# Loads, first sums, constants and the range flag: parts of a graph network kernel issued in another order

## The chip, the cores and the metric

The kernel runs on one core of one Trainium2 chip. A core has five engines, each with its own queue of instructions that it works through in order: TensorE (PE, matmul and transpose; its weight loads are listed as PEld), VectorE (DVE), ScalarE (ACT), GpSimd (POOL) and SyncE (SP, which only issues DMAs here). DMAs are issued from the queues of SP, ACT and POOL and moved by 16 DMA engines. A DMA's completion, and work on another engine, is waited for by a semaphore at the head of an instruction, and whatever stands behind that instruction on its engine waits too. The metric is the device time of one execution in microseconds (us), lower is better; of several executions the median is taken.

## What is computed

Sixteen graphs of 1024 nodes with 128 features, and a 0/1 adjacency `adj` of 1024 x 1024 each. Two layers, each with a residual and a normalization:

```python
# layer 0: a gated graph network of L = 4 steps
h = x
for i in range(L):
    hw = einsum('bnc,cd->bnd', h, weight[i])
    m  = einsum('bjn,bjd->bnd', adj, hw)
    h  = gru_cell(m, h, w_ih[i], w_hh[i], b_ih[i], b_hh[i])
x = layernorm(x + h * mask)

# layer 1: the adjacency is thinned row by row (each row's removals
# change later rows), then three SAGE layers and a linear head
adj_d = adj * dilate(adj > 0, mask)
def sage(x, Wr, Wx, b):
    agg = einsum('bij,bjd->bid', adj_d, x) / clip(sum(adj_d, -1), 1)
    out = agg @ Wr + x @ Wx + b
    return out / max(norm(out), 1e-12) * mask
h1 = bn(relu(sage(x,  Wr1, Wx1, b1)), g1, be1)     # bn: over all graphs and nodes
h2 = bn(relu(sage(h1, Wr2, Wx2, b2)), g2, be2)
h3 = bn(relu(sage(h2, Wr3, Wx3, b3)), g3, be3)
out = layernorm(x + (concat([h1, h2, h3]) * mask @ Wl + bl) * mask)
```

## The kernel before

P = C = 128, N = 1024, NB = 8 row tiles to a graph, HF = 512 columns (half a graph), B = 16 graphs, L0 = 4 GRU steps. A graph's adjacency is eight tiles of 128 x 1024 float32 (512 KB each). The order of the work on every engine is the order in which the program is written (a manual schedule for all five engines); the schedule adds the semaphore waits.

**The GRU pass** (`Gated`, to about 1329 us) works on two streams of graphs (even and odd), layer by layer in turn. A stream holds a graph's features as a high part and a low part (`hi`, `lo`: names h_hi, h_lo) so that sums over the adjacency are matmuls in a fast format; `layer` first makes the sums m = adj x (hi + lo) (line L1080, 32 matmuls of 128 x 512 into two banks, the first half of the columns, then the second), copies them (L1083), then makes the gates (L1092) with sigmoid, tanh and so on from ACT, DVE and POOL. `aside(n)` is called at fixed places in a layer and puts the other stream's work, and one step of the thinning, there. A stream's start for a graph is: load_x and load_adj (L1009, L1004, both from POOL's queue), `begin_rows` (hi by ACT L1044, lo by POOL L1045) and `begin(0)`, `begin(1)` (transposes of x, L1037).

**The thinning** (`FixPoint.steps`, a generator) is woven into it. A step loads four f_a tiles (L683, four graphs), takes their diagonal blocks (transposes L767 into f_pd), scans the rows on DVE (L735, prefix counts), derives parameters (L886 on ACT among them) and products (f_x, L893), and multiplies with f_tri on PE (L901). Further lines (L775, L863 and so on) repeat the removal for the block.

**The start** of the program: `make_consts` (identity, nodemask as nm_in, L613; mask, L618; first, L623), the first stream's x and eight h_a tiles on POOL's queue, all weights of the GRU on ACT's queue (`load_weights`, L953 to L961), four f_a tiles on SP's queue, `begin_rows`, then `prepare`: PE transposes every weight (L972, L975), multiplies (L979), and ACT and DVE copy the results. Weights of the four steps come in the tiles h_ms, h_r, h_z, h_zh. The second stream's x and h_a are then issued on POOL's queue, and `begin(0)` and the first nine steps of the thinning precede the first layer.

**The first Sage pass** (`Sage.first`, about 1329 to 1900) runs through slots (b, t), b = -1 to 15, t = 0 to 15. In a slot, unit (b + 1, t) of the next graph makes one of 16 blocks of the thinned adjacency (p_u, matmuls L1482, L1488, L1489 from p_nr and four p_a tiles; ACT makes p_at, L1490; POOL packs it, L1497), while for graph b PE aggregates (p_ag, L1561) and the layer follows. SP's queue carries the loads (p_nr L1466, p_a L1458, p_s L1472) and stores. `load_given` (20 loads of the Sage weights and vectors and three of the mask) is issued behind graph 0's loads. In slot (-1, 9) `constants` makes small tables on DVE and POOL: among them a copy of the identity (`drop`), and a row of ones that three DMAs store to rho (L1290). In slot (0, 1) `first_weights` multiplies the first Wr with drop (L1297), transposes the vectors (L1300) and copies the mask (mask48). A check on DVE (L1506) looks at each p_a tile for values that the fast way can't take, and writes to `bad`.

**The second and third passes** are the two further SAGE layers; in the third (about 2165 to 2286), iteration i takes up one unit (b, f), with transposes (L1411) of the unit three before. **The last part** (to 2365) makes the head and the normalization, graph by graph: eight blocks of 128 x 128 of a graph (k = 0 to 7; 0 to 3 from y in SBUF, 4 to 7 from one bank of PSUM) are scaled by POOL (k = 0), ACT (L1925) and, in the last graph, also DVE (L1923), and stored by SP (L1926).

**The flag.** `flagged` reduces `bad` on DVE (l_max), sums over partitions on PE (l_sum, L1964), makes 0 or 1 (l_flag, L1966), and every engine loads it to a register (L1967). If it is not 0, a general version would run; it is 0 here.

Of the kernel before, what the change touches and what calls it, by code (L numbers as in the profile page):

```python
# [8 lines left out]
F32 = mybir.dt.float32  # L9
# [12 lines left out]
P = 128  # L22
# [604 lines left out]
class FixPoint:  # L627
# [110 lines left out]
    def steps(self):  # L738

        nc, G = self.nc, self.G  # L740
        for c in range(G):
            self.load(c)
        old = None
# [173 lines left out]
class Gated:  # L917
# [27 lines left out]
    def load_weights(self):  # L945

        nc, wk = self.nc, self.wk
        weight, w_ih, w_hh, b_ih, b_hh = self.given
        self.w = wk.tile([P, 4, P], F32, name="h_w")
        self.w_in = {}  # L950
        names = iter(n for n in "h_ms h_r h_z h_zh".split() for _ in range(2))
        for l in range(L0):
            nc.scalar.dma_start(self.w[:, l, :], weight[l])  # L953
            for n, src in enumerate((w_ih, w_hh)):
                t = wk.tile([C, HF], F32, name=next(names))
                t = self.w_in[l, n] = t[:, :3 * C].rearrange("p (g c) -> p g c", g=3)
                nc.scalar.dma_start(t, src[l].rearrange("(g p) c -> p g c", p=C))
        t = wk.tile([P, NB, C], F32, name="h_x", bufs=3)
        self.b_in = [t[:L0 * 3, i, :] for i in range(2)]
        for t, src in zip(self.b_in, (b_ih, b_hh)):  # L960
            nc.scalar.dma_start(t, src.rearrange("l (g c) -> (l g) c", c=C))  # L961

# [28 lines left out]
    class Stream:  # L991
# [48 lines left out]
        def begin_rows(self, b):  # L1040
            x = self.x[b]
            for f in range(2):
                rows = slice(4 * f, 4 * f + 4)
                self.nc.scalar.copy(self.hi[:, rows, :], x[:, rows, :])  # L1044
                self.nc.gpsimd.tensor_tensor(self.lo[:, rows, :], x[:, rows, :],  # L1045
                                             self.hi[:, rows, :].bitcast(F32), ALU.subtract)

# [13 lines left out]

    def layer(self, st, l, aside):

# [5 lines left out]
        pm = [bank() for f in range(2)]  # L1069
        ms = []  # L1070
        for f in range(2):
            for n, part in enumerate((st.hi, st.lo)):
                if (f, n) != (0, 1):
                    aside(2 * f + n)
# [49 lines left out]
    def run(self, steps):  # L1124

        streams = [self.stream(s) for s in range(2)]
        first, second = streams
        first.load_x(first.b)
        for j in range(NB):
            first.load_adj(first.b, j)  # L1130
        self.load_weights()
        next(steps)
        first.begin_rows(first.b)
        self.prepare()
        second.load_x(second.b)
        for j in range(NB):
            second.load_adj(second.b, j)

        first.begin(0)
        for n in range(9):  # L1140
            next(steps)
        for b0 in range(0, B, 2):
            for l in range(L0):
                for s in range(2):
                    st, ot = streams[s], streams[1 - s]
                    self.layer(st, l, self.beside(st, ot, l, s, b0, steps))
        last = streams[1]
        for f in range(2):
            last.finish(f)
        for _ in steps:  # L1150
            pass
# [45 lines left out]
class Sage:  # L1197
# [61 lines left out]
    def constants(self):  # L1259
# [16 lines left out]
        nc.vector.memset(self.r6[:, C:], 0.0)  # L1276
        work = self.wk.tile([P, NB, C], F32, name="p_rl", bufs=1)

        mask, junk = self.cst["mask"], work[:, 0, :].rearrange("p (a b) -> p a b", a=NB)
        nc.vector.scalar_tensor_tensor(junk, mask, 0.0, mask, op0=ALU.is_gt, op1=ALU.not_equal,  # L1280
                                       accum_out=self.bad[:, BAD - 1:BAD])

        drop = work[:, 1, :]
        nc.vector.tensor_copy(drop, ident)
        nc.vector.memset(drop[:1, :], -1.0)
        nc.vector.memset(drop[:1, :1], 0.0)
        o = work[:B, 4:, :].bitcast(BF).rearrange("p a b -> p (a b)")
        nc.vector.memset(o, 1.0)
        for i in range(3):
            nc.sync.dma_start(self.rho[:, 3 + i, :], o)  # L1290
        self.drop = drop

    def first_weights(self):
        nc, ident = self.nc, self.cst["ident"]
        bank = lambda: self.ps1.tile([P, 4, P], F32, name="s_tr")[:, 0, :]
        w = bank()
        nc.tensor.matmul(w, self.drop, self.wr[:, 0, :], start=True, stop=True)  # L1297
        nc.vector.tensor_copy(self.wr[:, 0, :], w)
# [116 lines left out]
    def first(self):  # L1415

        nc, tc, cst = self.nc, self.tc, self.cst
        with ExitStack() as c:
# [22 lines left out]
            for k in range(4, NB):  # L1441
                self.load_a(0, k)
            self.load_given()
            self.eps = self.const([P, 1], 1e-5, "s_eps")
# [4 lines left out]
            for t, v in ((self.xh, 1.0), (self.xl, 0.0)):  # L1449
                nc.vector.memset(t[:, :, :1].bitcast(F32), v)  # L1450
            for b in range(-1, B):
                for t in range(16):
                    self.slot(b, t)
# [146 lines left out]
    def slot(self, b, t):  # L1600
# [82 lines left out]
        if nxt:  # L1683
            if t == 10:
                nc.sync.dma_start(self.at8[n, 0], self.g[n]["b", 0])
            if t == 13:
                nc.sync.dma_start(self.x1[n], self.g[n]["s"])
        if (b, t) == (-1, 9):
            self.constants()
        if (b, t) == (0, 1):  # L1690
            self.first_weights()
# [138 lines left out]
    def third(self):  # L1830

        nc, tc = self.nc, self.tc
        with ExitStack() as c:
# [9 lines left out]
            units = [(b, f) for b in range(B) for f in range(2)]  # L1843
            for i in range(len(units) + 3):

                if i >= 3:
# [20 lines left out]
    def last(self, r48):  # L1867
        nc, tc, cst = self.nc, self.tc, self.cst
        with ExitStack() as c:
# [42 lines left out]
            def norm(b):  # L1912
# [4 lines left out]
                for k in range(NB):  # L1917
                    src = pp[:, k - 4, :] if k > 3 else y[:, k, :]
                    scale, shift = rs[:, 0, k:k + 1], rs[:, 1, k:k + 1]
                    if k == 0:  # L1920
                        nc.gpsimd.tensor_scalar(y[:, k, :], src, scale, shift, op0=ALU.mult, op1=ALU.add)
                    elif b == B - 1 and k % 2 == 0:
                        nc.vector.tensor_scalar(y[:, k, :], src, scale, shift, op0=ALU.mult, op1=ALU.add)  # L1923
                    else:
                        nc.scalar.activation(y[:, k, :], src, AF.Identity, bias=shift, scale=scale)  # L1925
                nc.sync.dma_start(rows_of(self.out[b]), y)  # L1926

# [25 lines left out]

def flagged(tc, one, bad):

    nc = tc.nc
    with tc.tile_pool(name="l_wk", bufs=1) as wk, tc.tile_pool(name="l_ps", bufs=1, space=PSUM) as ps:
        t = wk.tile([P, 1], F32, name="l_max")
        nc.vector.tensor_reduce(t, bad, axis=AX.X, op=ALU.max)
        nc.vector.tensor_scalar(t, t, 0.0, None, op0=ALU.not_equal)  # L1960
        col = wk.tile([P, 1], F32, name="l_col")
        nc.vector.memset(col, 1.0)
        pt = ps.tile([P, 1], F32, name="l_sum")
        nc.tensor.matmul(pt[:1], t, col, start=True, stop=True)  # L1964
        f = one.tile([1, 1], I32, name="l_flag")
        nc.vector.tensor_scalar(f, pt[:1], 0.5, None, op0=ALU.is_gt)  # L1966
    return nc.values_load(f[0:1, 0:1], min_val=0, max_val=1,  # L1967
                          skip_runtime_bounds_check_because="0 or 1 by is_gt")

# [19 lines left out]
def kernel(ctx: ExitStack, tc: tile.TileContext, x, adj, nodemask,  # L1989
# [7 lines left out]
    with ExitStack() as ctx:  # L1997
# [3 lines left out]
        with ExitStack() as c:  # L2001
# [3 lines left out]
            gru.run(fix.steps())  # L2005
        Sage(ctx, tc, cst, adj, not_r, summed, nodemask, W, vec, Wl, bl, out, bad).run()
    with tc.If(flagged(tc, one, bad) > 0):
        general(tc, cst, x, adj, nodemask, weight, w_ih, w_hh, b_ih, b_hh, W, vec, Wl, bl, out)
# [31 lines left out]
```

## Time and profile before

Eight runs: median 2373.18 us, 2370.76 to 2377.78. One further execution was taken with the profiler:

| | |
|---|---|
| profiled execution, its own time | 2375.67 us |
| its span in the profile | 2373.8 us |
| granted TensorE clock, mean | 0.983 |
| busy: PE, DVE, ACT, POOL | 2267.8, 1909.9, 1373.7, 1021.5 us |
| DMA, mean over the span | 184 GB/s |
| POOL loads x: issued, then h_a from | 1.38, 5.58 us |
| ACT's first work other than issuing | 23.42 us |
| first sum on PE | 34.02 us |
| last wait of PE for p_a at the passage to Sage | ends 1365.75 us |
| the flag's register loads | 2365.0 us |

How it is read. The span runs from the first to the last instruction that the profile holds; 1.9 us lie outside. Lines of the timeline give: start and duration in us, engine, line of the kernel, operation, what is written from what, the size, how many alike (x), and in brackets how long the engine stood idle before and what released it; a group's duration covers all of its members. SPq, ACTq and so on are an engine's queue: DMA issues and register loads, which are not counted as busy. Windows give busy time of an engine within a stretch. "PE clock" is the clock granted to TensorE, 1.00 being full.

### The profile page before, as it was taken

The page shows a single profiled execution, that of the slowest core. Times are in us where ns is not written, and L with a number is a line of the kernel's source. Part 1 is how long each engine was busy: PE and PEld are TensorE (multiplying, and loading weights), DVE is VectorE, ACT ScalarE, POOL GpSimd, SP SyncE. Part 2 cuts the span into 40 slices and gives each one's busy share as a digit, 9 for nine tenths or more (in the row PEclk, how much of TensorE's full clock was granted, in tenths as well). Part 3 has the DMA queues.
Part 4 walks back from the last instruction along what each step waited for, and adds up shares of the span by engine and source line. Part 5 has one row for each costly group of instructions (what it writes and reads, how often), then busy time and mean ns, then how long its engine had stood idle before and what let it go on. Part 6 is the DMA issues. An engine that isn't in the chain of part 4 may idle for free.

```text
span 2373.8 us, 35696 instructions
## 1 busy us (share of the span) xinstructions
PE 2267.8 (96%) x11929; PEld 1563.3 (66%) x11945; DVE 1909.9 (80%) x4130; ACT 1373.7 (58%) x3209; POOL 1021.5 (43%) x963
## 2 busy tenths in 40 slices
PE   6999999999999999999999699999999989999987
PEld 4665655666655656556555477777777778887865
DVE  4998998998989989989899877777777566665876
ACT  3556565656465656565665556666666545555756
POOL 3335254263262452543532446766666434441002
PEclk9999999999999999999999799999999999999989
DMA  7337244373362462633740777777777277774414
GB/s 263 112 97 263 72 170 170 115 233 128 102 215 94 135 229 74 211 121 116 232 133 25 257 274 276 264 293 289 278 263 295 103 248 244 243 239 158 141 39 135
DMA packets 214389, 436.17 MB, mean 184 GB/s; under 512 B 59570, under 2 KB 80724, under 8 KB 214196
## 3 DMA queue, kind: packets, MB, share of 16 engines
q1 hardware_dynamic: 186756, 345.96, 42.3%
q0 software_dynamic: 23040, 83.90, 10.4%
q10 hardware_dynamic: 4400, 3.95, 0.5%
q8 instruction: 96, 1.57, 0.3%
q14 instruction: 97, 0.79, 0.1%
HBM read 324.49 MB, written 109.25 MB: 183 GB/s over the span
## 4 chain that ended last, share of the span: by engine, by line
PE 61%; DVE 15%; ACT 9%; DMA 7%; issue 4%; POOL 3%; SPq 0%; DVEq 0%; POOLq 0%; ACTq 0%
PE h_g L1092 14%; PE h_g L1080 11%; PE p_ag L1561 10%; PE q_ag L1797 5%; DVE f_rank L735 4%; PE q_ob L1764 3%; DMA h_a<-in_adj_dram 2%; DMA e_sum<-h_x 2%; PE p_u L1488 2%; PE p_u L1489 2%; PE p_u L1482 2%; PE s_tr L1411 2%; ACT s_junk L1389 2%; DVE f_a L727 2%; PE q_oa L1758 2%
## 5 line engine op out<-in xcount | busy, mean ns | idle before, releaser
L1092 PE MATMUL h_g<-h_h,h_wh 128*128 128x512 f32 x768 | 397.7, 599 | 3.2 <-DVE h_r L1105 3.0
L1092 PE MATMUL h_g<-h_ms,h_wi 128*128 128x512 f32 x768 | 392.2, 592 | 0.0
L1497 POOL CAST p_b<-p_at 128x512 uint8<-128x512 f32 x256 | 251.9, 1003 | 138.3 <-ACT p_at L1490 130.4
L735 DVE TENSOR_TENSOR_SCAN f_rank<-f_a,f_first,f_pd 128x1024 f16<-128x1024 f32 x128 | 299.2, 2343 | 3.3
L1080 PE MATMUL h_g<-h_a,h_hi 128*128 128x512 f32 x1024 | 285.1, 418 | 7.2 <-DMA h_a<-in_adj_dram 7.1
L1490 ACT ACTIVATE p_at<-p_u,s_less 128x512 fp32r<-128x512 f32 x256 | 175.8, 688 | 158.6 <-PE p_u L1489 153.8
L1092 PEld LDWEIGHTS h_g<-h_ms,h_wi 128*128 128x128 f32 x768 | 145.6, 190 | 184.0 <-issue 160.9
L1121 POOL TENSOR_TENSOR h_h<-h_zh,h_r 128x512 f32<-128x512 f32 x126 | 182.0, 1445 | 195.0 <-DVE h_r L1120 172.9
L1080 PE MATMUL h_g<-h_a,h_lo 128*128 128x512 f32 x1024 | 264.3, 395 | 0.0
L1080 PEld LDWEIGHTS h_g<-h_a,h_hi 128*128 128x128 f32 x1024 | 188.4, 188 | 72.0 <-issue 20.1
L863 DVE SCALAR_TENSOR_TENSOR f_nr<-f_u,f_q,f_a 128x1024 bf16<-128x1024 f16 x128 | 184.0, 1455 | 57.0 <-ACT f_u L912 50.4
L1115 POOL TENSOR_TENSOR h_zh<-h_z,h_h 128x512 f32<-128x512 f32 x63 | 80.4, 1276 | 323.7 <-ACT h_z L1111 323.7
L1080 PEld LDWEIGHTS h_g<-h_a,h_lo 128*128 128x128 f32 x1024 | 190.0, 188 | 39.4
L1506 DVE SCALAR_TENSOR_TENSOR p_a<-p_a 128x1024 bf16<-128x1024 f32 x128 | 209.3, 1671 | 2.7 <-DMA p_a<-in_adj_dram 2.7
L1389 ACT ACTIVATE s_junk<-s_o 128x128 bf16<-128x128 f32 x384 | 113.8, 298 | 134.5 <-DVE s_o L1382 134.5
L1092 PEld LDWEIGHTS h_g<-h_h,h_wh 128*128 128x128 f32 x768 | 129.1, 190 | 86.3 <-issue 67.2
L1083 ACT COPY h_ms<-h_g 128x512 f32<-128x512 f32 x128 | 73.9, 577 | 176.4 <-PE h_g L1080 132.6
L1108 ACT ACTIVATE h_r<-h_r,h_bi 128x512 f32<-128x512 f32 x128 | 92.4, 722 | 138.6 <-DVE h_r L1107 138.6
L1488 PE MATMUL p_u<-ident_b,p_a 128*128 128x128 bf16 x1024 | 144.9, 222 | 13.9 <-DMA p_a<-in_adj_dram 12.9
L909 ACT ACTIVATE f_u<-f_rank,f_q 128x128 f16<-128x128 f16 (+7 forms) x128 | 110.6, 867 | 74.9 <-DVE f_rank L849 74.9
L1489 PE MATMUL p_u<-ident_b,p_nr 128*128 128x128 bf16 x1024 | 144.9, 222 | 0.0
L1764 PE MATMUL q_ob<-s_wxp,q_xt 128*128 128x256 f32 x512 | 131.2, 400 | 0.0
(258 smaller groups left out, 4947.8 us busy)
## 6 DMA issues: line engine op xcount, KB each, us to landing
h_a<-in_adj_dram POOLq DMA_DIRECT2D x128, 512.0 KB, 7.5
p_a<-in_adj_dram SPq DMA_DIRECT2D x128, 512.0 KB
f_a<-in_adj_dram SPq DMA_DIRECT2D x124, 512.0 KB
e_nr<-f_nr SPq DMA_DIRECT2D x128, 256.0 KB
p_nr<-e_nr SPq DMA_DIRECT2D x32, 1024.0 KB
s_at<-p_b SPq DMA_DIRECT2D x32, 512.0 KB
s_ag<-s_ag SPq DMA_DIRECT2D x64, 256.0 KB
q_agi<-s_ag SPq DMA_DIRECT2D x32, 512.0 KB
```

The lines of the kernel that those rows point to most:

```text
L735: nc.vector.tensor_tensor_scan(out, a, other[:, 0, 0:1].to_broadcast([P, N]), start, op0=ALU.add, op1=ALU.bypass)
L863: nc.vector.scalar_tensor_tensor(nr, self.us[g], self.q[:, 2, g:g + 1], self.a[g], op0=ALU.not_equal, op1=ALU.is_ge)
L1080: nc.tensor.matmul(pm[f], part[:, j, :], st.adj[j][:, half[f]], start=(j == 0 and n == 0), stop=(j == NB - 1 and n == 1))
L1092: nc.tensor.matmul(pg, lhs, rhs, start=(i == 0), stop=(i == len(mm) - 1))
L1121: aid.tensor_tensor(h, zh, r, ALU.subtract)
L1488: nc.tensor.matmul(pu[:, i * P:(i + 1) * P], a[:, blk, 1], ib, start=False, stop=False)
L1489: nc.tensor.matmul(pu[:, i * P:(i + 1) * P], nr[:, k, blk], ib, start=False, stop=(i == 3))
L1490: nc.scalar.activation(g["at"][:, j, cols], pu, AF.Relu, bias=self.less2)
L1497: self.nc.gpsimd.tensor_copy(g["b", f][:, j, :], g["at"][:, j, f * HF:(f + 1) * HF].bitcast(F32))
L1506: self.nc.vector.scalar_tensor_tensor(low, a, 0.0, a, op0=ALU.is_gt, op1=ALU.not_equal, accum_out=self.bad[:, c:c + 1])
L1561: self.nc.tensor.matmul(pa, hi[:, j, :], at[:, j, f * HF:(f + 1) * HF], start=(start and n == 0), stop=(stop and n == len(js) - 1))
L1764: nc.tensor.matmul(pb[:, i], g["xt"][:, f, blk], self.wxp, start=False, stop=(i % 2 == 1))
```

## The change

Five edits, all in the order of issue or in the engine that takes a piece; the arithmetic is the same.

- *Start.* f_a's first four loads are issued by ACT and the GRU weights by SP; POOL issues both streams' x and then both streams' h_a at once, ahead of everything else. The low part of x in `begin_rows` goes to DVE for graph 0 (POOL for all others). `begin(0)` comes ahead of `prepare`. In the first layer of the first graph the sums go tile by tile (four matmuls for each h_a tile, both halves and both parts), `begin(1)` before them, and the first nine steps of the thinning are called (`lead`) after four tiles, the asides 0 to 3 with the last four.
- *Sage constants.* `constants` is called ahead of the slots. The drop matrix is written to wr2, scratch goes to wxp, and the row of ones is mask48, set to 1.0 for the purpose.
- *Sage loads.* `load_given` goes from behind graph 0's loads to slot (-1, 11), the three stores of ones to rho to slot (-1, 15), `first_weights` from slot (0, 1) to slot (0, 3).
- *Flag.* `flagged` is called in the third pass at i = 8, with a bank of the transposes' pool, and the register loads at i = 16.
- *Last graph's normalization.* POOL takes k = 0 and 1, ACT k = 2, DVE k = 3 to 7 (before: DVE 2, 4, 6, ACT the odd ones), and the store is two halves, the second by SP and the first by ACT.

```diff
@@ FixPoint.steps
         for c in range(G):
-            self.load(c)
+            self.load(c, nc.scalar)
@@ Gated.load_weights (also for w_ih, w_hh and the biases)
-            nc.scalar.dma_start(self.w[:, l, :], weight[l])
+            nc.sync.dma_start(self.w[:, l, :], weight[l])
@@ Stream.begin_rows
-                self.nc.gpsimd.tensor_tensor(self.lo[:, rows, :], x[:, rows, :],
-                                             self.hi[:, rows, :].bitcast(F32), ALU.subtract)
+                aid = self.nc.gpsimd if b else self.nc.vector
+                aid.tensor_tensor(self.lo[:, rows, :], x[:, rows, :],
+                                  self.hi[:, rows, :].bitcast(F32), ALU.subtract)
@@ Gated.layer
+        if (st.b, l) == (0, 0):
+            st.begin(1)
+            for j in range(NB):
+                if j == NB // 2:
+                    lead()
+                if j >= NB // 2:
+                    aside(j - NB // 2)
+                for n, part in enumerate((st.hi, st.lo)):
+                    for f in range(2):
+                        nc.tensor.matmul(pm[f], part[:, j, :], st.adj[j][:, half[f]],
+                                         start=(j == 0 and n == 0), stop=(j == NB - 1 and n == 1))
         for f in range(2):
             for n, part in enumerate((st.hi, st.lo)):
+                if (st.b, l) == (0, 0):
+                    continue
@@ Gated.run
         first.load_x(first.b)
-        for j in range(NB):
-            first.load_adj(first.b, j)
+        second.load_x(second.b)
+        for st in streams:
+            for j in range(NB):
+                st.load_adj(st.b, j)
+        next(steps)
         self.load_weights()
-        next(steps)
         first.begin_rows(first.b)
+        first.begin(0)
         self.prepare()
-        second.load_x(second.b)
-        for j in range(NB):
-            second.load_adj(second.b, j)
-
-        first.begin(0)
-        for n in range(9):
-            next(steps)
+        def lead():
+            for n in range(9):
+                next(steps)
@@ Sage.constants
-        drop = work[:, 1, :]
+        drop = self.wr2
         nc.vector.tensor_copy(drop, ident)
         nc.vector.memset(drop[:1, :], -1.0)
         nc.vector.memset(drop[:1, :1], 0.0)
-        o = work[:B, 4:, :].bitcast(BF).rearrange("p a b -> p (a b)")
-        nc.vector.memset(o, 1.0)
-        for i in range(3):
-            nc.sync.dma_start(self.rho[:, 3 + i, :], o)
+        nc.vector.memset(self.mask48[:B, :], 1.0)
@@ Sage.first
-            self.load_given()
...
+            self.constants()
             for b in range(-1, B):
@@ Sage.slot
-        if (b, t) == (-1, 9):
-            self.constants()
-        if (b, t) == (0, 1):
+        if (b, t) == (-1, 11):
+            self.load_given()
+        if (b, t) == (-1, 15):
+            for i in range(3):
+                nc.sync.dma_start(self.rho[:, 3 + i, :], self.mask48[:B, :])
+        if (b, t) == (0, 3):
             self.first_weights()
@@ Sage.third
+                if i == 8:
+                    pt = self.ps2.tile([P, 4, P], F32, name="s_tr")
+                    flag = flagged(nc, self.one, pt[:1, 0, :1], self.bad)
+                if i == 16:
+                    self.flag = nc.values_load(flag[0:1, 0:1], ...)
@@ Sage.last
-                    if k == 0:
+                    if k == 0 or (b, k) == (B - 1, 1):
                         nc.gpsimd.tensor_scalar(y[:, k, :], src, scale, shift, op0=ALU.mult, op1=ALU.add)
-                    elif b == B - 1 and k % 2 == 0:
+                    elif b == B - 1 and k > 2:
                         nc.vector.tensor_scalar(y[:, k, :], src, scale, shift, op0=ALU.mult, op1=ALU.add)
...
-                nc.sync.dma_start(rows_of(self.out[b]), y)
+                if b < B - 1:
+                    nc.sync.dma_start(rows_of(self.out[b]), y)
+                else:
+                    nc.sync.dma_start(rows_of(self.out[b])[:, 4:, :], y[:, 4:, :])
+                    nc.scalar.dma_start(rows_of(self.out[b])[:, :4, :], y[:, :4, :])
```

## The prediction

> **What bounds the kernel now.** I read the page's head first, then the chain of waits, then windows over each place that the change touches, and last the timeline of the engines there.
>
> ```profile
> span 2373.8 us, 35696 instructions
> PE 2267.8 (96%) x11929; PEld 1563.3 (66%) x11945; DVE 1909.9 (80%) x4130; ACT 1373.7 (58%) x3209; POOL 1021.5 (43%) x963
> PE 61%; DVE 15%; ACT 9%; DMA 7%; issue 4%; POOL 3%; SPq 0%; DVEq 0%; POOLq 0%; ACTq 0%
> ```
>
> TensorE is busy for 2267.8 of 2373.8 us, so all that can be won without removing matmuls is 106 us of PE gaps (and matmuls run at a lower clock). The change removes no matmul. It must be priced at the gaps: the start (0 to 34 us), the passage from the GRU pass to the first Sage pass (1320 to 1372), and the end (after 2361). Windows of the start (columns: length; busy us of PE, PEld, DVE, ACT, POOL; PE clock, DMA share, GB/s):
>
> ```profile
> 5.00:10.00 5.00, 1.73 (x7) 1.29 (x7) 0.86 (x3) 0.00 (x0) 4.30 (x8) 1.00 1.08 335
> 10.00:15.00 5.00, 0.90 (x3) 0.50 (x3) 0.56 (x1) 0.00 (x0) 0.00 (x0) 1.00 1.10 394
> 25.00:30.00 5.00, 3.72 (x14) 3.12 (x15) 1.14 (x3) 2.56 (x6) 4.59 (x6) 1.00 0.40 82
> ```
>
> The DMA engines are full until about 27 us, PE has little to do, then they fall idle. The passage, PE alone:
>
> ```profile
> 1350.00:1352.00 2.00, 0.68 (x7) 1.00 1.00 362
> 1354.00:1356.00 2.00, 0.00 (x0) 0.50 1.01 405
> 1366.00:1368.00 2.00, 2.00 (x7) 0.50 1.00 410
> ```
>
> PE stops at 1350.5 for some 15 us, its clock falls to 0.50 meanwhile, and it is still 0.50 when work resumes.
>
> **Part 1, the start.**
>
> ```profile
> 23.42 1.28 ACT L1044 ACT_TABLE_LOAD   x1 [23.42 <-DMA h_z<-in_L_gnn_w_hh_dram]
> 27.18 1.49 PE L972 MATMUL h_g<-ident,h_zh 128*128 128x128 f32 x6
> 34.02 2.10 PE L1080 MATMUL h_g<-h_a,h_hi 128*128 128x512 f32 x8
> 48.76 0.39 PE L901 MATMUL f_pd<-f_tri,f_x 128*128 128x128 bf16 x4
> ```
>
> ACT issues the 14 weight and bias loads and is blocked in them until 23.42, so its first high part is late; POOL stands behind that for the low part (2.49 us for two) and issues the second stream's loads only from 27.86. PE gets the last weight at 27.18 and starts the sums T0 = 34.0, so T0 is 6.8 after the last weight: transposes, eight products L979 (28.68 to 33.02), biases, begin(0).
> After: SP issues the weights, ACT four f_a tiles and then its high parts, POOL both x and 16 h_a. But every h_a issue still waits for the mask on DVE (L623), and the two new DVE subtractions stand ahead of that mask in DVE's order. They need ACT's high parts, those the landing of x (8.5) and the table load. So h_a, issued from 5.58 before, is issued from about 13.5 (8.5 + 1.28 + 1.14 + two DVE operations of 0.69, as a 128x512 tensor_tensor of L1058 takes, and the mask chain of about 1): the DMA works on f_a, x and weights alone until then. Those are 4 x 512, 2 x 512, 8 x 192 and 4 x 64 KB = 4.98 MB. At 0.385 MB/us (from the windows) and from 2 us they'd be in at 15; SP's issues wait for f_a landings in turn (as ACT's weight issues did: 12.27 and 17.38 for the last two), so I take the last weight at 18 and begin(0) already done: T0 = 18 + 6.5 = 24.5.
> Here a rule speaks against the change. The row: before, all 8.7 MB queued before 27 us are in when the last weight is, at a full DMA. The Trainium skill, "DMA: Bandwidth & Descriptors", section "Issuing engines are not separate DMA queues", says that transfers issued by different engines run interleaved on the same 16 engines, and that more issuers save only issue time. By it the first stream's 4.2 MB of h_a share the way: 9.2 MB / 0.385 + 2 = 25.8, T0 = 32.3. By the rows I keep 18, since h_a is held back until the smaller loads are nearly through; 32.3 goes into the range.
> The sums: 32 matmuls take 8.1 us either way, tile by tile or half by half. h_a at 13.5 + 1 of issue, 4.2 MB at 0.385, is in by about 27, while the sums run to 32.6, so arrival hardly stops them. But FixPoint's first part (lead) stood ahead of the sums (f_pd, L767, at 33.67) and now stands after four tiles, at T0 + 4.1. Behind L767 lie on DVE four scans (9.05 us), the parameters, ACT's L886 (1.95) and L893, ending at 48.16, 14.5 after L767. What is late next is L901 on PE: it can go at T0 + 4.1 + 14.5 + 0.3 = T0 + 18.9, while PE comes to it at T0 + 14.7 (48.76 now). PE waits 4.2 us, with the gates of its own stream behind it. Now 48.76, then T0 + 18.9: gain 29.9 - T0 = 5.4 us.
> A second rule bears on this wait. In the rows the clock fell to 0.50 some 3 us after PE stopped at 1350.5, and the first eight L1561 afterwards took 3.76 instead of 2.07; yet in the start the clock row is 1.00 through gaps of 5 us. The Trainium skill, "TensorE: Matmul & The Clock Gate", section "What's actually happening", lets an idle window of about 3.4 us halve the clock for the next window: 1.7 us lost by it, 0 by the start's row. I take 1.0: head -4.4 us. Range -7 (T0 22.5) to +3.4 (T0 32.3, 1 cold). Moving the low part off POOL is nothing by itself: POOL's 2.49 and DVE's 1.4 both lie before T0. The second stream's earlier loads are wanted only at about 50 and gain nothing.
>
> **Part 2, the passage.**
>
> ```profile
> 1350.31 5.32 DVE L1284 COPY p_rl<-ident 128x128 f32<-128x128 f32 x1
> 1357.08 1.25 SPq L1290 DMA_DIRECT2D s_rho<-p_rl  x3
> 1365.90 3.76 PE L1561 MATMUL p_ag<-p_at,p_xh 128*128 128x512 f32 x8
> 1366.18 0.69 ACT L1490 ACTIVATE p_at<-p_u,s_less 128x512 fp32r<-128x512 f32 x1 [15.17 <-PE p_u L1489]
> ```
>
> SP is in order. load_given's 20 small loads and 3 mask loads hold it from 1326.15 to 1345.36; only then come graph 1's p_nr, p_s and two p_a; then the three rho stores wait 8.9 us for DVE's ones, which stand behind a copy that takes 5.32 beside POOL's casts (the like one of ident, L608, 0.30); p_a(1,2) is issued at 1358.43 and p_a(1,3) at 1359.37; PE's last p_a wait ends at 1365.75.
> After: p_nr(1), p_s(1) and p_a(1,0..3) come ahead of load_given, the constants run while DVE waits for p_s (gaps 1.83 and 3.80 before 1333.1; without the slow copy they take about 2), rho reads a memset done long before. The p_a buffers are released by PE and DVE's checks at 1335 to 1345, the DMA moved only 48 GB/s in 1340 to 1345, so graph 1's 4.6 MB (2 p_nr and p_s 2.6, p_a 2.1) are in by about 1349, and the first unit can run when PE gets there, at 1350.4. Gone: 15.35 of wait and 1.85 of cold clock (units and L1561: 4.6 us from 1365.75 instead of 2.75), 17.2 in all.
> What is late next: load_given, now from about 1346. It took 19.2; 13 small ones took 4.9 with a quiet DMA, the first seven about 1.3 each beside bulk loads. I take 7 x 1.3 + 16 x 0.4 = 15.5, to 1361, and landing. first_weights is put off to slot (0,3), at 1350.4 + 3 x 2.8 = 1359, so PE may wait 3 us there; the rest of p_a(1,...) follows on SP at 1362 to 1366 for a slot at 1372, and POOL's low part of x, ready at 1353.3, costs up to 0.7. 17.2 - 3.7 = 13.5 us gained. Range: 17 (load_given at 0.4 each) to 5 (19.2 us and a later start: 10 of wait, 2 cold).
>
> **Part 3, the flag in the third pass, and the end.**
>
> ```profile
> 2250.19 0.60 PE L1411 MATMUL s_tr<-ident,s_r 128*128 128x128 f32 x4
> 2251.47 0.68 DVE L1864 TENSOR_TENSOR s_acc<-q_ob,s_acc 128x512 f32<-128x512 f32 x1
> ```
>
> In the third pass units follow each other every 3.79 us with PE and DVE without gaps. The new l_sum stands ahead of PE's transposes of unit 8, but DVE makes its operand after the unit before: s_acc until 2252.15, then reduce, compare, memset (0.27 + 0.13 + 0.06): 2252.6. PE, there at 2250.2, waits 2.3; behind it are its transposes, and ACT, for them. At i = 16 each engine loads the flag (0.46 to 0.57, all at once): 0.4 more. +2.7, range 0.5 (later slack takes it) to 3.5.
>
> ```profile
> 2363.61 0.41 DVE L1923 TENSOR_SCALAR u_y<-u_p,u_rs 128x128 f32<-128x128 f32 x1 [2.51 <-ACT u_y L1925]
> 2364.57 0.19 PE L1964 MATMUL l_sum<-l_col,l_max 128*1 128x1 f32 x2 [6.29 <-ACT u_y L1925]
> L1967 SPq TENSOR_LOAD <-l_flag x1: 486/486/486, 2365.0 to 2365.0; - x1
> ```
>
> Now DVE and ACT take turns to 2364.5, then l_sum, flag and load end at 2365.5. After, DVE does five of the eight (5 x 0.41 from about 2360.1), ACT one, POOL two; both stores are issued by about 2363.3 and the branch follows at once. The 8.3 us behind the branch stay. -2.1, range -0.5 to -3.5.
>
> **The sum.** -4.4 - 13.5 + 2.7 - 2.1 = -17.3 on the profiled execution of 2375.67 us (1.9 of it outside the span): 2358.4. The median shown is 2373.18, 2.5 lower: 2356, 0.7% less. A measurement tells 0.2%, 4.7 us, from no change.
>
> **Rivals.**
> *The stall only moves (chance 0.2).* load_given takes its 19.2 us behind the bulk loads; for it speaks that its issues were 1.3 to 3.8 us apart beside them, against it that the DMA is quieter after 1350. PE waits 10 at first_weights and restarts cold: the passage gives 5, the sum is -9: 2364.
> *The three queues share (0.13).* By the first rule T0 is 32.3, the head +3.4: -9.5, 2363.5. That the change doesn't do what it says is part of it: the tile order gains nothing, since weights and not rows set T0, and h_a starts later, not at once.
> *More comes off (0.1).* T0 22, no wait at first_weights, the flag's wait taken up: -7 - 17 + 1 - 3 = -26: 2347.
> *Slower (0.05).* Weight packets starve: all 13.4 MB that POOL, ACT and SP queue, the second stream's 4.2 too, pass before the last weight: 13.4 / 0.385 + 2 = 36.8, T0 43.3, head 43.3 - 29.9 + 1 = +14.4, and the sum is +1.5: 2374.7. It decides from T0 = 41.8, each us after costing one. Against it: POOL starts at 13.5, when most of the weights are in.
>
> **How the numbers follow.** The forecast has 0.52 with its own range 2351 to 2361. The rivals at 2363 to 2364 must lie inside and the ends of half of the case below it: 2349 to 2366. Faster by over 0.2% (under 2368.5) holds in all cases but the last and the worst of the two before it: 0.90; within 0.2%: 0.06; slower: 0.04.
>
> **What would show it.** The first sum near 24.5 and the last weight at 18, h_a issued from 13, not 5.6; a PE wait of 4 us at the first L901's place; no 15-us gap of ACT before p_at at 1350, but a small one of PE at the transposes and products of first_weights; one PE wait of over 2 us for l_max in the third pass; branch loads gone from the end. It is wrong if T0 is above 30, if the passage keeps a gap of over 6 us, or if later passes, untouched here, change by more than 2 us.

## The result and the profile after

The changed kernel takes 2368.24 us in the median of 11 runs (2363.23 to 2373.80), against 2374.78 us for the kernel before (32 runs, 2370.76 to 2377.78): 0.9971 of it, 95% interval 0.9964 to 0.9979, or 6.5 us less. The sign was right, but 2368.24 lies 2.2 us above the range's upper end, and the gain is 6.5 us where 17.3 were forecast. The profiled execution was among the fastest of its runs: 2363.89 us, span 2361.8. From the page of the changed kernel:

```profile
PE 2268.1 (96%) x11928; PEld 1562.8 (66%) x11945; DVE 1906.9 (81%) x4134; ACT 1373.0 (58%) x3206; POOL 1027.3 (43%) x962
```

No engine's work changed by more than 6 us. What moved is gaps, so I follow one engine's shared instructions: how much later (+) or earlier (-) than in the profile of before the same DVE instruction starts, in five profiles. Each column is one execution; the labels are those of the experiments below (e0 is the changed kernel again, in e1 to e3 one part is undone).

| stretch (time in before) | changed | e0 | e1 start undone | e2 passage undone | e3 flag undone |
|---|---|---|---|---|---|
| start, to 106 us | +1.9 | +4.0 | -0.5 | +2.6 | +6.1 |
| rest of the GRU pass, to 1333 | -2.2 | -2.2 | -2.4 | -2.7 | 0.0 |
| passage, to 1393 | -9.6 | -9.2 | -8.9 | +1.1 | -8.9 |
| first and second pass, to 2190 | -1.6 | 0.0 | -2.2 | -2.6 | -2.0 |
| flag in the third pass, to 2251 | +2.7 | +5.9 | +5.9 | +2.7 | -0.4 |
| rest and end | -3.4 | -2.6 | -2.6 | -3.1 | -0.5 |
| span | -12.0 | -4.2 | -10.7 | -2.0 | -5.8 |

The two long stretches that no edit touches, the rest of the GRU pass and the first and second passes, differ by up to 2.7 us from one execution to the next; the single execution of before is on the slow side there. In stretches of that length a difference of less than 3 us between two profiles says nothing.

**The start.** Timeline of the changed kernel:

```profile
13.04 4.29 POOL L1004 DMA_DIRECT2D h_a<-in_adj_dram  x8 [9.01 <-DVE first L623]
15.89 0.88 PE L972 MATMUL h_g<-ident,h_z 128*128 128x128 f32 x6
24.28 0.87 PE L972 MATMUL h_g<-ident,h_zh 128*128 128x128 f32 x3 [3.59 <-DMA h_zh<-in_L_gnn_w_hh_dram]
30.71 0.71 PE L1083 MATMUL h_g<-h_a,h_hi 128*128 128x512 f32 x2
49.02 0.38 PE L901 MATMUL f_pd<-f_tri,f_x 128*128 128x128 bf16 x4 [3.40 <-DVE f_x L893]
50.16 1.91 PE L1108 MATMUL h_g<-h_ms,h_wi 128*128 128x512 f32 x2
```

ACT is free 17 us sooner (6.80 instead of 23.42) and h_a is issued at 13.04, as worked out. But the last weight comes at 24.28, not 18; T0, the first sum, is 30.7, not 24.5; PE waits 3.40 us for f_x at L901; and behind that wait a pair of L1108 takes 1.91 us instead of 1.02. The clock's rows, with the same columns as in the prediction, show where it was halved:

```profile
20.00:25.00 5.00, 1.41 (x7) 1.04 (x7) 0.56 (x1) 0.00 (x0) 1.85 (x4) 0.50 1.14 398
50.00:55.00 5.00, 5.00 (x12) 2.25 (x11) 4.08 (x12) 3.55 (x7) 1.27 (x1) 0.66 0.00 0
```

**The passage.** PE alone, windows of 2 us (length, busy us, clock, DMA share, GB/s), then lines of all engines from the timeline:

```profile
1352.00:1354.00 2.00, 0.90 (x6) 1.00 0.54 156
1354.00:1356.00 2.00, 2.00 (x6) 0.51 0.03 7
1368.00:1370.00 2.00, 2.00 (x6) 0.50 1.02 402
```

```profile
1353.11 0.23 PE L1501 MATMUL p_u<-ident_b,p_a 128*128 128x128 bf16 x1 [2.27 <-DMA p_a<-in_adj_dram]
1354.00 2.42 DVE L1519 SCALAR_TENSOR_TENSOR p_a<-p_a 128x1024 bf16<-128x1024 f32 x1
1344.61 8.28 POOL L1510 CAST p_b<-p_at 128x512 uint8<-128x512 f32 x5
1346.36 0.33 SPq L1698 DMA_DIRECT2D s_at<-p_b  x1
1346.79 0.37 SPq L1471 DMA_DIRECT2D p_a<-in_adj_dram  x1
1361.90 0.30 ACT L1533 ACTIVATE p_rs<-p_mv,s_eps 128x8 f32<-128x8 f32 x1 [3.59 <-DVE p_mv L1530]
1363.81 0.25 PE L1567 MATMUL s_tr<-s_one,p_rl 1*128 1x1 f16 x4 [1.09 <-ACT p_rl L1560]
1366.15 0.22 PE L1313 MATMUL s_tr<-ident,s_vr 10*128 10x10 f32 x1 [0.96 <-DVE s_wr L1311]
```

The gap of 15 us is gone. Two smaller ones stand in its place. One is 2.85 us (0.58 and 2.27) for graph 1's last two p_a tiles, the last of them issued only at 1346.79 and landed at 1353.1. The other is 3.1 us in five waits between 1362.7 and 1367.2, at the row sums and at first_weights. Behind each of the two the clock is 0.50 for 3.4 us.

**The flag and the end:**

```profile
2184.07 0.19 PE L1988 MATMUL s_tr<-l_col,l_max 128*1 128x1 f32 x2 [1.98 <-DVE l_col L1987]
2354.11 1.71 SPq L1952 DMA_DIRECT2D out_dram<-u_y  x1
```

PE waits 1.98 us for the flag's operands. At the end the last normalization and both issues follow without taking turns, and the register loads are gone from there.

### The profile page after: what moved, and what is told of

Read it like the earlier page. It is cut to its first block, busy times and chain, and to the rows that moved or that the text cites. A ratio compares the mean times of both kernels' runs of the same rounds, so it can differ in the third digit from the quotient of the medians.

```text
span 2361.8 us, 35716 instructions
## 1 busy us (share of the span) xinstructions
PE 2268.1 (96%) x11928; PEld 1562.8 (66%) x11945; DVE 1906.9 (81%) x4134; ACT 1373.0 (58%) x3206; POOL 1027.3 (43%) x962
## 3 DMA queue, kind: packets, MB, share of 16 engines
q0 software_dynamic: 23040, 83.90, 10.2%
## 5 line engine op out<-in xcount | busy, mean ns | idle before, releaser
L1108 PE MATMUL h_g<-h_h,h_wh 128*128 128x512 f32 x768 | 398.6, 601 | 3.1 <-DVE h_r L1121 3.0
L1108 PE MATMUL h_g<-h_ms,h_wi 128*128 128x512 f32 x768 | 393.0, 593 | 0.0
L1510 POOL CAST p_b<-p_at 128x512 uint8<-128x512 f32 x256 | 258.9, 1031 | 123.8 <-ACT p_at L1503 123.8
L1096 PE MATMUL h_g<-h_a,h_hi 128*128 128x512 f32 x1008 | 280.1, 418 | 5.6 <-DMA h_a<-in_adj_dram 5.6
L1108 PEld LDWEIGHTS h_g<-h_ms,h_wi 128*128 128x128 f32 x768 | 145.9, 190 | 184.5 <-issue 161.9
L1519 DVE SCALAR_TENSOR_TENSOR p_a<-p_a 128x1024 bf16<-128x1024 f32 x128 | 212.7, 1703 | 0.0
L1108 PEld LDWEIGHTS h_g<-h_h,h_wh 128*128 128x128 f32 x768 | 129.4, 191 | 86.6 <-issue 66.5
```

The costliest lines, as they stand in the source:

```text
L1096: nc.tensor.matmul(pm[f], part[:, j, :], st.adj[j][:, half[f]], start=(j == 0 and n == 0), stop=(j == NB - 1 and n == 1))
L1108: nc.tensor.matmul(pg, lhs, rhs, start=(i == 0), stop=(i == len(mm) - 1))
L1510: self.nc.gpsimd.tensor_copy(g["b", f][:, j, :], g["at"][:, j, f * HF:(f + 1) * HF].bitcast(F32))
L1519: self.nc.vector.scalar_tensor_tensor(low, a, 0.0, a, op0=ALU.is_gt, op1=ALU.not_equal, accum_out=self.bad[:, c:c + 1])
```

## The experiments

Each group of kernels ran on one chip, beside runs of the kernel before on that chip. In the first group that was 2374.61, in the second 2375.17, in the third 2376.15 us; I compare distances to it. By the intervals given with the ratios a distance is known to about 3 us each way, so two distances that lie less than about 4 us apart may be the same.

**The changed kernel again, and one part undone at a time.** e0 is the kernel itself.

> The changed kernel itself, as the measure for the others of this group. It was 2368.24 us (2363.2 to 2373.8), 6.5 under before. Theory: the profiled execution of it (2363.9) had the passage to Sage 9.3 us shorter, the third pass 2.8 longer, the end 3.1 shorter and the start 1.6 longer; the same in another execution within 1 us each, and a median of 2368. Rival: what the passage gains depends on the execution (transfers, clock windows), so another profile shows that term off by 3 us or more and the others the same.

2368.52 us, 6.1 under before, ratio 0.9970 (0.9958 to 0.9982). Its profile is 7.8 us longer in span than the first one. The terms that differ are not the passage, as the rival had it, but the start (+2.1), the flag (+3.2) and the untouched first and second passes (+1.6).

e1 takes back the start: queues, h_lo, order of the first sums, lead.

```diff
-        second.load_x(second.b)
-        for st in streams:
-            for j in range(NB):
-                st.load_adj(st.b, j)
-        next(steps)
+        for j in range(NB):
+            first.load_adj(first.b, j)
         self.load_weights()
+        next(steps)
...
-            nc.sync.dma_start(self.w[:, l, :], weight[l])
+            nc.scalar.dma_start(self.w[:, l, :], weight[l])
```

> All of the change but the start (queues, h_lo, order of the first sums, lead). Theory: the start costs 1.6 us, as the lag of the changed kernel behind before at 75 to 160 us says, so this one is 1 to 2 us faster than the changed one: about 2366.5. Rival 1: the start's edits gain later in the GRU pass (the lag has gone to -0.6 us at 1290): then it is slower by about 0.6: 2369. Rival 2, my prediction's term: slower by 4.4: 2372.6.

2364.70 us, 9.9 under before (0.9952, 0.9939 to 0.9966): 3.8 faster than e0. By the medians alone that is at the edge of what can be told (the two intervals overlap), but the profiles say the same: the columns with the new start read +1.9, +4.0, +2.6 and +6.1, the one without it -0.5. The start's edits cost time, and nothing of it comes back later.

e2 takes back the passage.

```diff
             for k in range(4, NB):
                 self.load_a(0, k)
+            self.load_given()
...
-        if (b, t) == (-1, 11):
-            self.load_given()
+        if (b, t) == (-1, 9):
+            self.constants()
...
-        if (b, t) == (0, 3):
+        if (b, t) == (0, 1):
             self.first_weights()
```

> All of the change but the passage (constants, load_given, the rho stores and first_weights where they were). Theory: the passage is the one large gain, 9.3 us by the traces: 2377.5, slower than before by 2 to 3. Rival, if the medians' 6.5 is right for the whole and the profile was lucky: the passage is worth only 4 to 5 us: 2373.

2379.35 us, 4.7 over before (1.0016, 1.0006 to 1.0026), 10.8 slower than e0 (its profiled execution, 2373.82 us, was one of its fastest). Without the passage the change as a whole would have been a loss.

e3 takes back the flag, made and loaded behind the last part, with the new normalization kept.

```diff
-                if i == 8:
-                    pt = self.ps2.tile([P, 4, P], F32, name="s_tr")
-                    flag = flagged(nc, self.one, pt[:1, 0, :1], self.bad)
-                if i == 16:
-                    self.flag = nc.values_load(flag[0:1, 0:1], ...)
...
-    with tc.If(sage.flag > 0):
+    with tc.If(flagged(tc, one, bad) > 0):
```

> All of the change but the flag, which is made and loaded after the last part as before, behind the new division of the last normalization. Theory: the third pass gets its 2.8 us back and the end loses 1 to 2 (sum, flag and load one after another): 2366.5 to 2367.5. Rival: the third pass takes the wait up in a chain that has slack, and the flag at the end costs 2.5: 2370.5.

2369.75 us, 4.9 under before (0.9981, 0.9973 to 0.9989), 1.2 slower than e0, within its interval of no difference. The third pass does get its time back (-0.4 in the table), and the end loses it again (-0.5 against -2.6 to -3.4). As it stands, moving the flag pays nearly nothing.

**The flag without PE's wait.** e5 makes the operands on DVE at i = 4 and leaves only the sum and the compare at i = 8.

```diff
+                if i == 4:
+                    t, col = flag_parts(nc, self.one, self.bad)
                 if i == 8:
                     pt = self.ps2.tile([P, 4, P], F32, name="s_tr")
-                    flag = flagged(nc, self.one, pt[:1, 0, :1], self.bad)
+                    flag = flagged(nc, self.one, pt[:1, 0, :1], t, col)
```

> The changed kernel with the flag's DVE part (maximum, compare, ones) at i = 4 of the third pass and only the sum on PE at i = 8, so that PE has nothing to wait for. Theory: the 1.97 us wait of PE is the whole cost, and where it lets the clock fall to 0.50 for 6.8 us it costs 5.9 instead of 2.7: so the third pass is 2.7 to 5.9 shorter, no clock of 0.50 between 2170 and 2270 in the profile, and the median falls 3 to 5 us, to about 2364.5. Rival: the five register loads at i = 16 cost more than half of it: it falls by less than 1.5.

2364.18 us, 11.0 under before (0.9957, 0.9944 to 0.9970): 4.9 better than e0's distance. The windows of PE around the flag (columns as above), first e0, then e5:

```profile
2184.00:2188.00 4.00, 2.04 (x10) 1.00 0.59 143
2188.00:2192.00 4.00, 4.00 (x20) 0.58 0.35 126
2192.00:2196.00 4.00, 4.00 (x16) 0.56 0.00 0
```

```profile
2184.00:2188.00 4.00, 4.00 (x27) 1.00 0.21 80
```

In e0 PE waits 1.96 us and then works 6.8 us at half clock. The first profile had a wait of 1.98 and no half clock. That is the 2.7 against 5.9 of the table: the same wait costs about twice as much in some executions. In e5 there is no wait and no half clock. Its third pass is 0.4 longer than before's and 0.8 longer than e3's, which has no flag there; that is all that is left for the sum and the register loads together.

**The scans' start.** e6 calls lead() ahead of the first sums.

```diff
-                if j == NB // 2:
+                if j == 0:
                     lead()
```

> The changed kernel with lead() called before the first tile's sums instead of after four. Theory: f_x is ready 3.8 us earlier against PE, the wait of 3.4 us at the first L901 goes, and with it the 3.4 us at clock 0.50 that follow it (1.7 lost): 5 us faster, 2363.5, and the start is then no longer slower than before's. Rival: PE gets there, but the first gates then wait elsewhere (ACT's L886 and the table load ahead of the sigmoid): gain of 1 to 2.

2362.39 us, 12.8 under before (0.9947, 0.9935 to 0.9960), 6.7 better than e0's distance; the theory's 5 or a little more. PE comes to L901 at 45.59 in this profile and finds f_x ready, the clock is not halved again in the start, and at 106 us the kernel is 2.9 us ahead of before. Yet the last weight was no earlier than in the other profiles, and the first sum came at 31.3: of the start's two faults this mends one.

**The checks.** e8 takes four checks of graph 1 out of the passage and makes them some slots later.

```diff
-            if t >= 12:
+            if t >= 12 and now:
                 self.check(n + 1, t - 12)
+            if b == 0 and 6 <= t < 10:
+                self.check(n, t - 6)
```

> The changed kernel with DVE's four checks of graph 1's first p_a tiles taken out of slots (-1, 12..15) and made in slots (0, 6..9). Theory: DVE, not a transfer, holds up the passage after 1353: 16 us of checks back to back, 1.7 to 2.4 each beside POOL's casts instead of 1.27, stand ahead of the statistics of graph 1 and so of ACT, the row sums and first_weights; PE's gaps of 4.5 us in 1362 to 1367 and the half clock after them (1.7) go: 4 to 6 us faster, 2363.5. Rival: load_given's last rows or p_a's landing are as late as DVE: under 1.5 us.

2363.70 us, 11.5 under before (0.9956, 0.9944 to 0.9968), 5.4 better than e0's distance. The passage is 12.9 us shorter than before's in its profile, against 8.9 to 10.8 in the eight profiles that have the changed passage as it stands. Windows of all engines (columns as in the prediction's first windows), first the changed kernel, then e8:

```profile
1355.00:1360.00 5.00, 5.00 (x30) 3.47 (x30) 5.00 (x8) 0.69 (x1) 5.00 (x4) 0.76 0.46 157
```

```profile
1355.00:1360.00 5.00, 4.74 (x37) 3.46 (x35) 2.49 (x9) 2.40 (x5) 2.36 (x4) 1.00 0.70 189
```

DVE had no free moment from 1340 to 1360 in the changed kernel; without the four checks it is half idle in the last 5 us, and PE stays at full clock. POOL gains too: with DVE idle from 1352.3 to 1355.1 a cast takes 0.57 us, where it took 1.66.

```profile
1352.37 3.40 POOL L1510 CAST p_b<-p_at 128x512 uint8<-128x512 f32 x6
```

PE's waits at the row sums and first_weights fall from 3.1 to 1.5 us, and the half clock behind them is gone, here and in e10 and e11 below, which have the same edit. That the clock stays full behind the wait for p_a as well is luck: PE still waits 2.8 us for it (2.9 in the changed kernel). In e10 and e11 that wait is 1.9 and 2.3 us, a half clock of 3.4 us follows it, and the passage is 11.3 and 11.0 us shorter than before's, not 12.9.

**The DMA engines shared.** e9 removes what held h_a back: the mask's scratch lay in memory that h_a's buffers reuse.

```diff
-        self.adjp = pool("h_adj", bufs=NB)
         self.one = pool("h_one", bufs=1)
+        self.adjp = pool("h_adj", bufs=NB)
```

> The changed kernel with two pools of the GRU pass allocated in the other order, so that h_a's buffers no longer lie over the mask's scratch and POOL issues h_a at about 4 us without a wait for DVE. Theory (the queues share the DMA engines): with h_a in flight from 4 us the last weight lands later, at 27 to 31 instead of 24 to 29, first sum at 34 to 37: 2 to 4 us slower than the changed one, 2371. Rival (h_a's late issue is what costs): all is in by 26, sums begin before 30: 2 to 3 us faster, 2365.5.

2380.41 us, 5.2 over before (1.0018, 1.0006 to 1.0031), 11.3 worse than e0's distance. With h_a issued from 4.0 us the last weight is used at 37.96 and the first sum starts at 44.5; by 38 us 13.45 MB have been moved, all that the three queues hold.

```profile
37.96 1.51 PE L972 MATMUL h_g<-ident,h_zh 128*128 128x128 f32 x6 [0.27 <-DMA h_zh<-in_L_gnn_w_ih_dram]
```

So loads that go out truly at once are slower by far than before's order, and more so than I had expected.

e7 puts f_a behind the weights, all on SP's queue, and leaves h_a held.

```diff
-            self.load(c, nc.scalar)
+            self.load(c)
...
-        next(steps)
         self.load_weights()
+        next(steps)
         first.begin_rows(first.b)
```

> The changed kernel with the four f_a loads issued by SP behind the weights instead of by ACT from 0.8 us. Theory: the last weight is late (24 to 29 us in the executions seen) because the weights' rows of 512 bytes share the DMA engines first with f_a, then with h_a; without f_a's 2.1 MB in front they are in before h_a starts, at 12 to 16, and the first sum comes at 20 to 22; the first L901 at 38 to 42 instead of 49 to 53: 7 to 10 us faster than the changed kernel, 2359 to 2361. Rival: SP's issues go on waiting for landings, h_a (from 12 us) overtakes the last matrices, and the last weight still lands after 20: 2 to 3 us.

2360.63 us, 15.5 under before (0.9931, 0.9915 to 0.9948), 9.4 better than e0's distance. SP's queue in the changed kernel and in e7:

```profile
5.98 0.49 SPq L953 DMA_DIRECT2D h_w<-in_L_gnn_weight_dram  x1
11.41 0.37 SPq L957 DMA_DIRECT2D h_z<-in_L_gnn_w_ih_dram  x1
14.15 0.49 SPq L957 DMA_DIRECT2D h_zh<-in_L_gnn_w_hh_dram  x1
```

```profile
8.01 0.49 SPq L957 DMA_DIRECT2D h_zh<-in_L_gnn_w_hh_dram  x1
10.67 1.83 SPq L683 DMA_DIRECT2D f_a<-in_adj_dram  x4
```

With f_a's 2.1 MB in front, SP stands still from 6.5 to 11.4 us, waiting for the landing of the first h_ms (4.9 us by the waits of its queue), and its last matrix goes out just as h_a begins. Without it the weights are all out at 8.5; PE transposes the last one at 15.0 and begins the sums at 19.1. From there on the sums do follow h_a's landings tile by tile, to 34. Only here and in e11 below, where the weights go first too, does PE wait for h_a at these sums at all; in the other nine profiles with this order of sums every tile is in before PE needs it.

**Together.** e10 has e5, e6 and e8; e11 adds e7.

> The changed kernel with the three repairs that were tried alone: flag's DVE part early, lead() before the sums, checks later. Theory: each takes out its own stall (4.3, 6.1 and 4.8 us alone, by medians) and they add up: 2353. Rival: the clock windows' luck was part of each, and together they give 11: 2357.

2356.28 us, 19.9 under before (0.9914, 0.9901 to 0.9927): 13.8 better than e0's distance. The three alone had 17.0 by the distances given above (15.2 as the theory summed them), the rival said 11. The measured value lies between, and an uncertainty of about 4 us does not tell which of them is right.

> The three repairs and the weights ahead of f_a. Theory: as the weights alone, less what lead() first then waits for f_a: 5 to 8 us under the three: 2346. Rival: with lead() first PE waits for f_a's landing (issued behind 14 weight loads, with h_a in flight) until 22 or later, and the two repairs of the start don't add: 2351.

2351.73 us, 24.4 under before (0.9902, 0.9889 to 0.9915), 4.5 better than e10. The start is 6.5 us shorter than e10's in the profiles and only 1.0 shorter than e7's. As the rival said, the start's two repairs don't add: f_a comes behind the weights, and with lead() first PE waits for it, 1.77 and then 2.29 us.

```profile
23.23 0.47 PE L767 MATMUL f_pd<-ident,f_a 128*128 128x128 f32 x1 [2.29 <-DMA f_a<-in_adj_dram]
```

It beats both kernels, by 1.0% and 0.7%.

## Why the prediction was wrong

**The last weight at 18 us: wrong, and the step that failed most.** The prediction counted f_a, x and the weights ahead of the last weight, without h_a, and allowed 3 us for SP's waits, because it took those loads to be nearly through when h_a starts. It set aside the rule that all issuers share the same DMA engines, which gave 25.8 and T0 = 32.3. In the first profile, e0, e2 and e3 the last matrix is used at 24.3 to 28.7 and the first sums start at 30.7 to 34.9, above the 30 that the prediction itself named as a sign of being wrong. The rule was right. h_a was held to 13, as I worked out, but one wait of SP cost 4.9 us before that, so the last matrices were still to be moved when h_a came. e7 shows the one end: with f_a behind the weights the last matrix is transposed at 15.0. e9 shows the other, 37.96, with 13.45 MB moved by then; the slower rival had 36.8 and 13.4 MB. So that rival's mechanism was real, and only h_a's accidental wait kept it out of the changed kernel.

**The wait at L901 and its cold clock: right.** 4.2 us forecast, 3.40 found, and half clock behind it. The forecast gave the cold clock 1.0 by halving between 1.7 and nothing; a half-clock stretch of 3.4 us follows the wait in both profiles of the changed kernel and in e2, e3, e5, e8 and e9. The "row of 1.00" that spoke against it is no evidence: six transposes L972 take 1.49 us in before's start under a clock shown as 1.00, and six of them 0.88 in the changed kernel at 15.89, so before's start ran at half clock too. In sum the head cost 3.8 us by e1, where a gain of 4.4 was forecast.

**The passage: right in kind, 8.9 to 9.6 us gained in the table's profiles (10.8 by e2's median) instead of 13.5.** The stall of 15.35 us and its cold restart went, but PE's five waits in that stall sum to only 13.9; the rest was work that still has to be done. What is late next was named wrongly: load_given took 10.0 us (1347.21 to 1357.25), not 15.5, and no wait of PE is put down to it. (It has 20 loads with the three of the mask, not 23. Its first seven lay 1.3 to 3.8 us apart in before, 14.4 in all, not 1.3 each; in the changed kernel they took 5.9.) Two other things were late.

The first is p_a(1,3), in at 1353.1 instead of 1349. SP works in order, and ahead of this load stands the store of p_b (L1698), which waited 3.2 us for POOL's cast, to 1346.3; DVE's check of graph 0's tile, which also had to be done, had ended at 1345.9. Whether load_given, issued right behind it, made its landing late as well (6.3 us) was not tried.

The second is DVE itself. The checks L1519 take 1.7 to 2.4 us beside POOL's casts, and the casts 1.66. In before, checks with POOL idle took 1.25 to 1.29, and four casts with DVE held up in a copy 0.57 each:

```profile
1353.26 2.28 POOL L1497 CAST p_b<-p_at 128x512 uint8<-128x512 f32 x4
1356.98 1.25 DVE L1506 SCALAR_TENSOR_TENSOR p_a<-p_a 128x1024 bf16<-128x1024 f32 x1
```

Alone, a check starts every 1.16 to 1.21 us and a cast every 0.57; together both start every 1.62 to 1.68 us, nearly the sum, as if the two took turns. Statistics, row sums and first_weights stood behind the checks. The prediction knew these checks only as what releases the buffers and put nothing for their time. The Trainium skill has the mechanism: "SBUF — State Buffer", section "Who interferes with whom", says that a VectorE instruction with two inputs in SBUF contends with a GpSimd instruction that reads SBUF. A check is such an instruction (it reads p_a twice) and a cast reads p_at, so the trace agrees. e8 shows that the checks were in the way (waits of 1.5 us where there were 3.1) and that the casts are short without them; that the port is the cause is argued from the rows, not tried.

**The flag: the wait right (2.3 forecast, 1.98), the price too small.** 2.7 was forecast and 2.7 found in the first profile (2.6 to 2.7 in e2, e8 and e9), but 5.9 in e0, e1, e6 and e7, because the wait can also halve the clock. e5, which has no such wait, returns 4.9 in the median.

**The end: right.** -2.1 forecast; -2.6 to -3.4 found, of which the flag's move is the larger part: e3, with the flag back at the end, keeps only -0.5.

With +3.8 for the start, -9.6 for the passage, +4.3 for the flag (between 2.7 and 5.9) and -3.0 for the end the sum is -4.5, near the -6.5 measured. By term, the start was 8.2 too good, the passage 3.9, the flag 1.6, the end 0.9 too bad. That the sign came out right rests on the passage: without it (e2) the kernel is 4.7 us slower than before. The chances were too sure of two independent sums; the case "the queues share" had 0.13 and was what happened, together with half a stall that moved.

## What to carry to other kernels

Loads that are issued at once don't arrive at once: order them by when their data is first needed, and look for the small ones among them: here a matrix of 192 KB took as long to land as a 512-KB tile in flight beside it. When a stall is to be removed, list what each engine has queued over that stretch, not only the queue that caused it, and price it by rows taken with the neighbour engine busy. A wait of 2 us on TensorE is to be priced twice, with and without the half clock behind it; the cheapest repair is often to make the operand a few steps sooner.

## What the runs showed of the hardware

A wait of 1.96 to 1.98 us on an otherwise fully busy TensorE was followed by 6.8 us at half clock in four profiles (e0, e1, e6, e7; the third pass 5.9 us longer than before's) and by none in four others (the first, e2, e8, e9; 2.6 to 2.7 longer). The prediction counted on an idle window of about 3.4 us for a half clock; 1.96 us of idle was enough in e0, and 2.2 in before, where the clock fell at 1352.85.

Where the wait falls goes with it. In all 13 traces the times from one change of clock to the next are multiples of 3.41 us. Counted in such steps from the last change, the wait lies inside one step in e0, e1, e6 and e7, and a step's end cuts it in the first profile (1.38 and 0.60 us), in e8 (1.65 and 0.31), in e9 (1.49 and 0.48), and in e2, where only 0.02 us lie beyond. Over all 13 traces no step at full clock with less than 1.49 us of PE idle was followed by a half clock, and every one with more than 2.0 us was; between these both occur. This is read from the traces; no run was made to test it.

A kernel with such waits can be expected to vary more from run to run. The record fits, but does not show it: the changed kernel has 10.6 us between the extremes of 11 runs, e10 with three such places mended 2.9, in only 5 runs.

Half-clock stretches last 3.4, 6.8, 10.2, 13.7 or 17.1 us in these profiles (the last one of each is cut off by the end). A matrix of 192 KB in rows of 512 bytes took 10 us to land beside h_a's 512-KB tiles (issued 14.15, used 24.28), about as long as the tiles themselves do there (10.2 in the median of the first 30 us). And before the first change of clock in a profile the row's 1.00 is no measurement, as the 1.49 and 0.88 us of the six transposes show.
